# Two row additions and the norms' reciprocal roots are divided anew between VectorE and GpSimd in a two-layer graph-attention and expert kernel

## The chip, the cores and the metric

The kernel runs on one core of one Trainium2 chip. A core has five engines that run side by side, each through its own list of instructions in order: TensorE (PE in the profile; its weight loads are PEld), VectorE (DVE), ScalarE (ACT), GpSimd (POOL) and SyncE (SP). They wait for each other by semaphores. In this kernel SP issues the plain transfers, and GpSimd issues the indirect ones, that is, those whose row addresses come from a tile. The metric is the device time of one execution in microseconds; lower is better.

## What is computed

The input x has 64 batches of 256 rows with 256 values, all float32. Two layers follow, each with attention over a fixed adjacency mask and then a feed-forward part. Every part works on the row-normalised x and is added to x:

```
x = x + elu(attention(layernorm(x), adj, 4 heads))
x = x + layernorm(x) @ weight.T + bias            # the dense layer
x = x + relu(attention(layernorm(x), adj, 1 head))
x = x + moe(layernorm(x))                         # 8 experts, the best 2 of each row
layernorm(x) = (x - mean) / sqrt(var + 1e-5)
```

So each batch has four norms: of the input, before the dense layer, before the second attention, and before the experts. The mixture of experts returns `tokens + sum of weight * expert(tokens)` over the two experts that a router picks for the row.

## The kernel before, in words

**Tiles.** A batch is held as a tile of 128 partitions by 2 row blocks by 256 values, 512 float32 values in each partition. The means need no subtraction, since the weights are centred once in the setup; a norm needs only the factor `rstd = (var + eps)^-0.5` for every row. `norm_stats` gets it: VectorE takes statistics of each row block (L290, L291), and then GpSimd does two instructions on a 128x2 tile, an addition of eps (L293) and a power with -0.5 (L294).

**The steps of a batch.** `batch_layers` is a generator, and each `yield` ends a step of the batch and names the rank that the next step has among all the work of its turn. Counted from 0, the steps that matter here are: 0, norm 1 (of the input x0) and a transposition; 1, the projection to q (L315), its exponentials on ScalarE with rstd as scale (L323) and its scaling on VectorE (L327); 2 and 3, the scores z (L346); 4, the weighted sums pv (L360) and hp; 5, x1 (L394 to L398); 6, x1b, which is x1 plus the bias (L401, on GpSimd), norm 2 and a transposition of x1; 7, the dense layer pf (L408), x2 (L414) and norm 3; 8 to 11, the second attention; 12, its rows rel on ScalarE (L431) and their addition to x2 (L434, on GpSimd); 13, norm 4; 14, the small factors `by` (L440, L443); 15, the normalised rows xng for the experts and the residual base (L449, L454); then the router's logits.

**The order.** The order of all instructions is written by the loop at the end of the kernel, under a manual schedule. A new batch begins at every third turn (`TICKS = 3`), so five or six batches are in work at one time, each at another step. In each turn every active job makes one step, in the order of their ranks. Batches go in chunks of 4 (twelve times), then of 2 (six times), then of 1 (twice); the last two batches are dense, that is, every expert is computed for them. At the end of a chunk, `route` works out on VectorE where each row goes, and `send` (L741) scatters the rows to a place in memory sorted by expert: two sends for each row block, spread over the turns on GpSimd's queue.

**Experts.** A pair is 256 sorted rows for one expert. `expert_pair` loads its rows xr (L599) and the expert's weights we (L610) by SP's queue; the load of xr waits for the sends that may lie in it. A pair's next steps are the transposition px (L617), a copy to sT on ScalarE (L621), the hidden layer ph (L649) and hT (L655), and the second product py (L664), to which VectorE adds a bias into the tile y (L670). ScalarE scales y (L642), and then `scatter` adds its rows to the output by two indirect transfers from GpSimd's queue (L681). One pair is scattered in a turn, and each scatter waits for the two transfers before it. A dense expert uses the same y tiles, and adds them to its own base (L707), which SP stores in the end (L714).

**Buffers.** A tile's `bufs` says how many copies of it exist; a new one waits for the reader of the oldest. Here y has 6, the tile "e" has 2, mv has 6, and rstd has 8.

Of the kernel before, what the change touches and what calls it, by code (L numbers as in the profile page):

```python
# [8 lines left out]
F32 = mybir.dt.float32  # L9
I32 = mybir.dt.int32  # L10
AF = mybir.ActivationFunctionType
ALU = mybir.AluOpType
AX = mybir.AxisListType

P = 128
# [11 lines left out]
def kernel(  # L27
# [17 lines left out]
    nc = tc.nc  # L45
    B, N, D = x.shape
# [4 lines left out]
    NT = N // P  # L51
    EPS = 1e-5
# [54 lines left out]
    nc.vector.memset(ones, 1.0)  # L107
    mean_w = const.tile([P, P], F32, tag="mean_w", name="mean_w")
    nc.vector.memset(mean_w, 1.0 / D)
    mhalf = const.tile([P, NT], F32, tag="mhalf", name="mhalf")  # L110
    nc.vector.memset(mhalf, -0.5)

    adj_i = work.tile([P, NT, N], adj.dtype, tag="z", name="adj_i", bufs=6)
# [25 lines left out]
    def gnn_weights(w, a, heads, slope, name):  # L139

        d = D // heads
        wx = const.tile([P, KT, heads, d + 3], F32, tag=name, name=name)
        for k in range(KT):
            nc.sync.dma_start(
                out=wx[:, k, :, :d],  # L150
                in_=w[k * P : (k + 1) * P, :].rearrange("p (h d) -> p h d", h=heads),
            )
        av = work.tile([P, 2, d], F32, tag="e", name=name + "_a")
        nc.scalar.dma_start(out=av.rearrange("p s d -> p (s d)"), in_=rows_to_all(a, 2 * d))
        prod = work.tile([P, heads, d], F32, tag="hp", name=name + "_p")
        for k in range(KT):
            for s, c in ((0, d + 1), (1, d)):
                nc.vector.tensor_mul(
                    prod, wx[:, k, :, :d], av[:, s : s + 1, :].to_broadcast([P, heads, d])
                )  # L160
                nc.vector.tensor_reduce(wx[:, k, :, c : c + 1], prod, AX.X, ALU.add)
            nc.vector.tensor_scalar(
                wx[:, k, :, d + 1 : d + 2], wx[:, k, :, d + 1 : d + 2], 1.0 - slope, None,
                op0=ALU.mult,
            )
            nc.vector.tensor_scalar(
                wx[:, k, :, d + 2 : d + 3], wx[:, k, :, d : d + 1], slope - 1.0, None,
                op0=ALU.mult,
            )
        flat = wx.rearrange("p k h c -> p k (h c)")  # L170
        center(flat, heads * (d + 3))
        return flat
# [29 lines left out]


    C_B1, WROW = KT * D, KT * D + 64
    WBUFS, XBUFS = 7, 5
    wpack = tc.dram_tile([E, P, WROW], F32, name="wpack")
    w2s = const.tile([P, E, KT * D], F32, tag="w2s", name="w2s")
    b2s = const.tile([P, E, D], F32, tag="b2s", name="b2s")
# [74 lines left out]

    def norm_stats(src):
        stats = small.tile([P, NT, 6], F32, tag="stats", name="stats")
        mv = small.tile([P, NT, 2], F32, tag="mv", name="mv", bufs=6)
        for t in range(NT):
            nc.vector.bn_stats(stats[:, t, :], src[:, t, :])  # L290
            nc.vector.bn_aggr(mv[:, t, :], stats[:, t, :])  # L291
        rstd = small.tile([P, NT], F32, tag="rstd", name="rstd", bufs=8)
        nc.gpsimd.tensor_scalar_add(rstd, mv[:, :, 1], EPS)  # L293
        nc.gpsimd.tensor_tensor(rstd, rstd, mhalf, ALU.pow)  # L294
        return mv, rstd

    def transposed(src, tag="xT", bufs=4):
        pt = bank("pt", [KT, N])
# [71 lines left out]
    def batch_layers(b, c0, xng, lg):  # L370

        x0 = xin.pop(b)
        if b + AHEAD < B:
            xin[b + AHEAD] = load_batch(b + AHEAD)
        _, rstd = norm_stats(x0)
        xT = transposed(x0)
        yield 20
        q = projected(xT, wx0, H, rstd)
        yield 10
        probs = []  # L380
        scores(q, H, range(0, 2), masks[0], probs)
        yield 10
        scores(q, H, range(2, 4), masks[0], probs)
        yield 50
        pvs, rinv = attended(q, H, probs)
        hp = work.tile([P, NT, D], F32, tag="hp", name="hp")
        for t, pv in enumerate(pvs):
            nc.vector.tensor_tensor(
                hp[:, t, :].rearrange("p (h d) -> p h d", h=H), pv[:, :, :HD],
                rinv[:, t, :, None].to_broadcast([P, H, HD]), ALU.mult,  # L390
            )
        yield 20
        ex = work.tile([P, NT, D], F32, tag="e", name="e")
        nc.scalar.activation(ex, hp, AF.Exp)  # L394

        x1 = work.tile([P, NT, D], F32, tag="x1", name="x1", bufs=2)
        nc.vector.scalar_tensor_tensor(x1, hp, 0.0, x0, op0=ALU.max, op1=ALU.add)
        nc.vector.scalar_tensor_tensor(x1, ex, 1.0, x1, op0=ALU.min, op1=ALU.add)  # L398
        yield 30
        x1b = work.tile([P, NT, D], F32, tag="x1b", name="x1b")  # L400
        nc.gpsimd.tensor_add(x1b, x1, bias_f[:, None, :].to_broadcast([P, NT, D]))  # L401
        _, rstd = norm_stats(x1)
        xT = transposed(x1)
        yield 70
        pf = bank("pf", [NT, D])
        for t in range(NT):
            for k in range(KT):
                nc.tensor.matmul(  # L408
                    pf[:, t, :], xT[:, k, t * P : (t + 1) * P], wfT[:, k, :],
                    start=(k == 0), stop=(k == KT - 1),  # L410
                )
        x2 = work.tile([P, NT, D], F32, tag="x2", name="x2", bufs=4)
        for t in range(NT):
            nc.vector.scalar_tensor_tensor(  # L414
                x2[:, t, :], pf[:, t, :], rstd[:, t : t + 1], x1b[:, t, :],
                op0=ALU.mult, op1=ALU.add,
            )
        _, rstd = norm_stats(x2)
        yield 60
        xT = transposed(x2)  # L420
        yield 20
        q = projected(xT, wx1, 1, rstd)
        yield 10
        probs = []
        scores(q, 1, range(1), masks[1], probs)
        yield 40
        pvs, rinv = attended(q, 1, probs)
        yield 5
        rel = work.tile([P, NT, D], F32, tag="rel", name="rel")
        for t, pv in enumerate(pvs):  # L430
            nc.scalar.activation(  # L431
                rel[:, t, :], pv[:, 0, :D], AF.Relu, scale=rinv[:, t, :]
            )
        nc.gpsimd.tensor_add(x2, x2, rel)  # L434
        yield 60
        mv, rstd = norm_stats(x2)
        yield 15

        by = small.tile([P, 2, NT], F32, tag="by", name="by")
        nc.vector.scalar_tensor_tensor(  # L440
            by[:, 0], mv[:, :, 0], -1.0, rstd, op0=ALU.mult, op1=ALU.mult
        )
        nc.vector.tensor_scalar(by[:, 1], rstd, 1.0, None, op0=ALU.add)  # L443
        yield 50
        xe = keep.tile([P, NT, ROW], F32, tag="xng", name="xng", bufs=XNG)
        dense = b >= ROUTED
        base = work.tile([P, NT, D], F32, tag="dbase" if dense else "base", name="base")
        for t in range(NT):
            nc.scalar.activation(  # L449
                xe[:, t, :D], x2[:, t, :], AF.Identity, bias=by[:, 0, t : t + 1],  # L450
                scale=rstd[:, t : t + 1],
            )
        for t in range(NT):
            nc.scalar.activation(  # L454
                base[:, t, :], x2[:, t, :], AF.Identity, bias=by[:, 0, t : t + 1],
                scale=by[:, 1, t : t + 1],
            )
        xng.append(xe)
        yield 35
        if not dense:  # L460
            d = nc.sync.dma_start(
                out=out_rows[b * N : (b + 1) * N, :].rearrange("(t p) d -> p t d", p=P), in_=base
            )
            tc.declare_no_dep(
                d.ins, query=SYNC, group="out", reason="no row is added to before its chunk has been sent"
            )
            tc.add_to_no_dep_group("out", d.ins)
            based.append(d.ins)
            nc.sync.nop()
        xT = transposed(xe[:, :, :D], *(("xTd", DENSE) if dense else ()))  # L470
        yield 50
        pl = bank("pl", [NT, E])
        for t in range(NT):
            for k in range(KT):
                nc.tensor.matmul(
                    pl[:, t, :], xT[:, k, t * P : (t + 1) * P], rT[:, k, :],
                    start=(k == 0), stop=(k == KT - 1),
                )
        nc.vector.tensor_copy(lg[:, c0 : c0 + NT, :], pl)
        if dense:  # L480
            dense_batch[b] = dict(base=base, xT=xT)
# [178 lines left out]
    def result(hT, e):  # L660
        py = bank("py", [2, D])
        for t in range(2):
            for f in range(KT):
# [2 lines left out]
                    w2s[:, e, f * D : (f + 1) * D].rearrange("p e c -> p (e c)"),  # L666
                    start=(f == 0), stop=(f == KT - 1),
                )
        y = io.tile([P, 2, D], F32, tag="y", name="y", bufs=6)
        nc.vector.tensor_add(y, py, b2s[:, e, :].to_broadcast([P, 2, D]))  # L670
        return y

# [225 lines left out]
    with tc.manual_schedule():  # L898
        while more or active or waiting or dense_jobs or scatters:
# [22 lines left out]
            order_steps.append(step)  # L922
            for entry in sorted(active, key=lambda a: a[:2]):
                entry[0] = next(entry[2], None)
            active[:] = [a for a in active if a[0] is not None]
            step += 1

# [34 lines left out]
```

## Time and profile before

| what | us |
|---|---|
| median of 3 runs | 1796.04 (1791.09 to 1798.93) |
| the profiled execution | 1822.89 |
| its span, first to last instruction | 1821.2 |
| TensorE busy (matmuls) | 1629.5 (89%) |
| VectorE busy | 1231.4 (68%) |
| ScalarE busy | 839.9 (46%) |
| GpSimd busy | 1084.2 (60%) |
| GpSimd: the two row additions, 64 each | 109.2 and 108.1 |
| GpSimd: the norms' two instructions, 256 each | 81.2 and 184.2 |
| GpSimd: scatters (262) and sends (248) | 419.4 and 261.2 |

Lines of the profile name the source line, the engine, the operation, and the tiles as output<-input. In tables by group the numbers after a count are busy us and mean ns of one, and behind the bar the idle time just before and who ended it. A timeline line has the start, the length, the instruction, and in brackets the idle time of its engine before it and what ended that. In tables of stretches each engine has its busy us and instructions, in the order PE, PEld, DVE, ACT, POOL, and then come the granted TensorE clock (1.00 is full speed), the transfers' share and GB/s. The profiled execution was slower than the median by 26.9 us; its mean granted clock was 0.937.

### The profile page before, as it was taken

To read this page: it belongs to the slowest core of one execution; us is meant where nothing else is said; L and a number is where in the kernel's file an instruction comes from. 1 tells how busy PE (TensorE), PEld (TensorE's weight loads), DVE (VectorE), ACT (ScalarE), POOL (GpSimd) and SP (SyncE) were. 2 spreads that over 40 slices of the span, in tenths; PEclk is the share of its full clock that TensorE was granted. 3 is DMA by queue.
4 is the path that set the end of the run, shared out by engine and by line. 5 is a ranking of instruction groups with operands and counts; after the bars stand their busy time and mean duration, and the time that the engine had idled before them with its cause. 6 is when DMAs were issued, how large, how long until landed. Compare 5 with 4: busy or idle time off the path is not lost. (4 is left out here: it accounts for less than half of the span.)

```text
span 1821.2 us, 30155 instructions
## 1 busy us (share of the span) xinstructions
PE 1629.5 (89%) x9254; PEld 1433.0 (79%) x9254; DVE 1231.4 (68%) x4680; ACT 839.9 (46%) x1773; POOL 1084.2 (60%) x1164
## 2 busy tenths in 40 slices
PE   6998889899999999999999999999989998778692
PEld 5787778788888888888878788887878887667582
DVE  6889887867685858686766768688678876522231
ACT  1243333355554555554545545555455545443241
POOL 1333645557575767767676757576685767644444
PEclk9999989899998999998989999999899989889897
DMA  4410211235344444544354534444353436576663
GB/s 137 140 36 24 71 60 53 79 109 121 105 95 104 109 126 108 132 103 110 93 119 112 119 91 95 118 111 128 84 127 101 107 82 166 118 186 139 135 139 43
DMA packets 137374, 192.90 MB, mean 106 GB/s; under 512 B 18680, under 2 KB 91392, under 8 KB 137216
## 3 DMA queue, kind: packets, MB, share of 16 engines
q1 hardware_dynamic: 86592, 122.61, 22.0%
q0 software_dynamic: 49632, 67.39, 20.6%
q8 instruction: 76, 1.25, 0.3%
q10 hardware_dynamic: 992, 0.99, 0.2%
q14 instruction: 82, 0.67, 0.1%
HBM read 101.77 MB, written 89.15 MB: 105 GB/s over the span
## 5 line engine op out<-in xcount | busy, mean ns | idle before, releaser
L681 POOL DMA_INDIRECT out_dram<-y,to x262 | 419.4, 1601 | 231.1 <-DMA out_dram<-y,to 103.5
L360 PE MATMUL pv<-q,z 128*128 128x65 f32 (+1 forms) x2560 | 394.4, 314 | 5.3 <-DVE z L346 5.0
L360 PEld LDWEIGHTS pv<-q,z 128*128 128x128 f32 x2560 | 364.9, 210 | 21.1 <-DVE z L346 5.4
L293 POOL TENSOR_SCALAR rstd<-mv 128x2 f32<-128x2 f32 x256 | 81.2, 317 | 376.2 <-DVE mv L291 355.6
L741 POOL DMA_INDIRECT xs<-xng,pos x248 | 261.2, 1053 | 68.2 <-issue 66.0
L315 PE MATMUL pq<-wx,xT 128*128 128x268 f32 (+1 forms) x1024 | 265.4, 402 | 35.8 <-ACT xT L305 31.8
L649 PE MATMUL ph<-sT,we 128*128 128x256 f32 x1048 | 252.6, 397 | 48.1 <-ACT sT L621 22.9
L346 DVE SCALAR_TENSOR_TENSOR z<-pd,q,mask 128x256 f32<-128x256 f32 x640 | 265.1, 473 | 9.9 <-PE pd L339 7.5
L649 PEld LDWEIGHTS ph<-sT,we 128*128 128x128 f32 x1048 | 205.0, 200 | 80.6 <-ACT sT L621 29.4
L664 PE MATMUL py<-w2s,hT 128*128 (+1 forms) x1176 | 265.4, 381 | 0.6 <-ACT hT L655 0.6
L315 PEld LDWEIGHTS pq<-wx,xT 128*128 128x128 f32 x1024 | 188.1, 194 | 85.8 <-ACT xT L305 50.6
L664 PEld LDWEIGHTS py<-w2s,hT 128*128 128x128 f32 x1176 | 220.5, 191 | 29.3 <-ACT hT L655 1.0
L305 ACT COPY xT<-pt 128x512 f32<-128x512 f32 x256 | 144.9, 589 | 192.8 <-PE pt L301 127.6
L327 DVE SCALAR_TENSOR_TENSOR q<-pq,rstd,q 128x256 f32<-128x256 f32 x256 | 112.4, 479 | 154.5 <-ACT q L323 150.7
L655 ACT ACTIVATE hT<-ph,we 128x256 f32<-128x256 f32 x294 | 123.3, 471 | 173.4 <-PE ph L649 122.9
L670 DVE TENSOR_TENSOR y<-py,b2s 128x512 f32<-128x512 f32 x147 | 96.7, 688 | 149.2 <-PE py L664 77.9
L294 POOL TENSOR_TENSOR rstd<-rstd,mhalf 128x2 f32<-128x2 f32 x256 | 184.2, 719 | 21.4
L642 ACT ACTIVATE y<-y,w 128x256 f32<-128x256 f32 x262 | 112.9, 498 | 177.5 <-DVE y L670 171.1
L290 DVE BATCH_NORM_STATS2 stats<-x 128x6 f32<-128x256 f32 x384 | 155.9, 406 | 0.0
L408 PE MATMUL pf<-wfT,xT 128*128 128x256 f32 x512 | 145.7, 435 | 0.1
L323 ACT ACTIVATE q<-pq,rstd 128x12 f32<-128x12 f32 (+1 forms) x256 | 56.5, 265 | 162.3 <-POOL rstd L294 150.8
L434 POOL TENSOR_TENSOR x<-x,rel 128x512 f32<-128x512 f32 x64 | 109.2, 1706 | 25.2 <-ACT rel L431 25.0
(147 smaller groups left out, 2259.2 us busy)
## 6 DMA issues: line engine op xcount, KB each, us to landing
we<-wpack SPq DMA_DIRECT2D x147, 288.0 KB
xr<-xs SPq DMA_DIRECT2D x131, 260.0 KB
xin<-in_x_dram SPq DMA_DIRECT2D x64, 256.0 KB
out_dram<-base SPq DMA_DIRECT2D x64, 256.0 KB
out_dram<-y,to POOLq DMA_INDIRECT x262
xs<-xng,pos POOLq DMA_INDIRECT x248
xs<-fill SPq DMA_DIRECT2D x9, 260.0 KB
wpack<-wt SPq DMA_DIRECT2D x8, 288.0 KB
```

Source lines behind the costliest of these rows:

```text
L290: nc.vector.bn_stats(stats[:, t, :], src[:, t, :])
L294: nc.gpsimd.tensor_tensor(rstd, rstd, mhalf, ALU.pow)
L305: nc.scalar.copy(dst, pt)
L315: nc.tensor.matmul(pq.rearrange("p h c -> p (h c)"), xT[:, k, t * P : (t + 1) * P], wx[:, k, :], start=(k == 0), stop=(k == KT - 1),)
L346: nc.vector.scalar_tensor_tensor(z[:, j, :], pd[:, i, :], q[:, j, h, d + 2 : d + 3], mask[:, j, :], op0=ALU.max, op1=ALU.mult,)
L360: nc.tensor.matmul(pv[:, h, :], z[:, j, t * P : (t + 1) * P], q[:, j, h, : d + 1], start=(j == 0), stop=(j == NT - 1),)
L408: nc.tensor.matmul(pf[:, t, :], xT[:, k, t * P : (t + 1) * P], wfT[:, k, :], start=(k == 0), stop=(k == KT - 1),)
L649: nc.tensor.matmul(ph[:, f, :], we[:, k * D + f * P : k * D + (f + 1) * P], xT[:, k, :], start=(k == 0), stop=(k == KT - 1),)
L655: nc.scalar.activation(hT[:, f, :], ph[:, f, :], AF.Gelu, bias=we[:, C_B1 + f : C_B1 + f + 1])
L664: nc.tensor.matmul(py[:, t, :], hT[:, f, t * P : (t + 1) * P], w2s[:, e, f * D : (f + 1) * D].rearrange("p e c -> p (e c)"), start=(f == 0 ...
L681: d = nc.gpsimd.indirect_dma_start(out=out_rows, out_offset=bass.IndirectOffsetOnAxis(ap=to[:, t : t + 1], axis=0), in_=y[:, t, :], in_off ...
L741: d = nc.gpsimd.indirect_dma_start(out=xs_d[: E * CAP * PAIR, :], out_offset=bass.IndirectOffsetOnAxis(ap=at, axis=0), in_=xe, in_offset=None,
```

## The change

GpSimd no longer adds rows. VectorE adds the bias (x1b) in step 5, straight behind x1, and adds the second attention's rows to x2 at the start of step 13, ahead of norm 4. In `norm_stats` the first norm of a turn leaves its statistics and its rstd in the first half of a double tile, the second norm uses the other half, and then one pair of GpSimd instructions on 128x4 serves both. A norm that finds no partner in its turn is finished alone at the turn's end. Norm 2 and norm 1 of two batches fall in one turn, in that order, and norm 4 and norm 3 of two others in another. The buffers follow: mv 4 and rstd 5 of the double size, "e" 1, which in the setup also holds the two attentions' vectors one after the other, and y 7.

```
-        mv = small.tile([P, NT, 2], F32, tag="mv", name="mv", bufs=6)
+        if half_done:
+            mv, rstd = half_done[0]
+            at = NT
+        else:
+            mv = small.tile([P, 2 * NT, 2], F32, tag="mv", name="mv", bufs=4)
+            rstd = small.tile([P, 2 * NT], F32, tag="rstd", name="rstd", bufs=5)
+            half_done.append((mv, rstd))
+            at = 0
         for t in range(NT):
             nc.vector.bn_stats(stats[:, t, :], src[:, t, :])
-            nc.vector.bn_aggr(mv[:, t, :], stats[:, t, :])
-        rstd = small.tile([P, NT], F32, tag="rstd", name="rstd", bufs=8)
-        nc.gpsimd.tensor_scalar_add(rstd, mv[:, :, 1], EPS)
-        nc.gpsimd.tensor_tensor(rstd, rstd, mhalf, ALU.pow)
-        return mv, rstd
+            nc.vector.bn_aggr(mv[:, at + t, :], stats[:, t, :])
+        if at:
+            finish_norms(2 * NT)
+        return mv[:, at : at + NT, :], rstd[:, at : at + NT]
+
+    def finish_norms(n):
+        mv, rstd = half_done.pop()
+        nc.gpsimd.tensor_scalar_add(rstd[:, :n], mv[:, :n, 1], EPS)
+        nc.gpsimd.tensor_tensor(rstd[:, :n], rstd[:, :n], mhalf[:, :n], ALU.pow)
...
+        x1b = work.tile([P, NT, D], F32, tag="x1b", name="x1b")
+        nc.vector.tensor_add(x1b, x1, bias_f[:, None, :].to_broadcast([P, NT, D]))
         yield 30
-        x1b = work.tile([P, NT, D], F32, tag="x1b", name="x1b")
-        nc.gpsimd.tensor_add(x1b, x1, bias_f[:, None, :].to_broadcast([P, NT, D]))
         _, rstd = norm_stats(x1)
...
-        nc.gpsimd.tensor_add(x2, x2, rel)
         yield 60
+        nc.vector.tensor_add(x2, x2, rel)
         mv, rstd = norm_stats(x2)
...
-        av = work.tile([P, 2, d], F32, tag="e", name=name + "_a")
+        av = work.tile([P, 2, d], F32, tag="e", name=name + "_a", bufs=1)
...
-        ex = work.tile([P, NT, D], F32, tag="e", name="e")
+        ex = work.tile([P, NT, D], F32, tag="e", name="e", bufs=1)
...
-    WBUFS, XBUFS = 7, 5
+    WBUFS, XBUFS, YBUFS = 7, 5, 7
...
-        y = io.tile([P, 2, D], F32, tag="y", name="y", bufs=6)
+        y = io.tile([P, 2, D], F32, tag="y", name="y", bufs=YBUFS)
...
             for entry in sorted(active, key=lambda a: a[:2]):
                 entry[0] = next(entry[2], None)
+            if half_done:
+                finish_norms(NT)
```

More of the change, by code (lines that the diff above doesn't have):

```diff
@@ L109 @@
     nc.vector.memset(mean_w, 1.0 / D)
-    mhalf = const.tile([P, NT], F32, tag="mhalf", name="mhalf")
+    mhalf = const.tile([P, 2 * NT], F32, tag="mhalf", name="mhalf")
     nc.vector.memset(mhalf, -0.5)
@@ L280 @@
     nc.vector.memset(scan_mask[:, :, 0:1], 0.0)
+    half_done = []
     def norm_stats(src):
         stats = small.tile([P, NT, 6], F32, tag="stats", name="stats")
-        mv = small.tile([P, NT, 2], F32, tag="mv", name="mv", bufs=6)
+        if half_done:
[6 more added lines that the diff above has]
+            at = 0
         for t in range(NT):
             nc.vector.bn_stats(stats[:, t, :], src[:, t, :])
-            nc.vector.bn_aggr(mv[:, t, :], stats[:, t, :])
-        rstd = small.tile([P, NT], F32, tag="rstd", name="rstd", bufs=8)
-        nc.gpsimd.tensor_scalar_add(rstd, mv[:, :, 1], EPS)
-        nc.gpsimd.tensor_tensor(rstd, rstd, mhalf, ALU.pow)
-        return mv, rstd
+            nc.vector.bn_aggr(mv[:, at + t, :], stats[:, t, :])
[6 more added lines that the diff above has]
+        nc.gpsimd.tensor_tensor(rstd[:, :n], rstd[:, :n], mhalf[:, :n], ALU.pow)
     def transposed(src, tag="xT", bufs=4):
```

## The prediction

> **What bounds the kernel now.** I read the page's busy shares first, then a table of stages (busy us and instructions by engine, granted TensorE clock), then the waits, then the timeline around them.
>
> ```profile
> PE 1629.5 (89%) x9254; PEld 1433.0 (79%) x9254; DVE 1231.4 (68%) x4680; ACT 839.9 (46%) x1773; POOL 1084.2 (60%) x1164
> ```
> ```profile
> 20.00:350.00 330.00, 293.24 (x1733) 254.23 (x1734) 270.50 (x937) 108.85 (x259) 144.63 (x204) 0.92 0.22 66
> 350.00:1240.00 890.00, 851.86 (x5021) 757.56 (x5020) 638.11 (x2392) 476.79 (x982) 605.02 (x645) 0.96 0.45 110
> 1240.00:1590.00 350.00, 309.49 (x1706) 272.85 (x1706) 252.86 (x1124) 177.90 (x366) 233.48 (x238) 0.92 0.47 113
> 1590.00:1780.00 190.00, 157.48 (x733) 136.11 (x733) 52.80 (x170) 71.18 (x159) 80.89 (x52) 0.91 0.64 148
> ```
>
> TensorE is busy 96% from 350 to 1240 us, so nothing off it counts unless it opens or closes one of its gaps. Its clock is only 0.96 there, though: at half speed for 8% of 890 us, some 71 us, so about 36 us lost besides 38 us of gaps. In that stage the waits put 18.5 us, in 13 pieces, on px (L617) waiting for xr. This is one such piece, at the end of a chunk of four batches:
>
> ```profile
> 819.50 1.86 POOL L434 TENSOR_TENSOR x<-x,rel 128x512 f32<-128x512 f32 x1
> 820.73 1.86 POOL L401 TENSOR_TENSOR x1b<-x,bias_f 128x512 f32<-128x512 f32 x1
> ...
> 823.87 0.71 POOL L294 TENSOR_TENSOR rstd<-rstd,mhalf 128x2 f32<-128x2 f32 x1
> 824.61 0.43 ACT L323 ACTIVATE q<-pq,rstd 128x12 f32<-128x12 f32 x2 [2.04 <-POOL rstd L294]
> ...
> 824.92 0.88 DVE L327 SCALAR_TENSOR_TENSOR q<-pq,rstd,q 128x256 f32<-128x256 f32 x2 [2.71 <-ACT q L323]
> ...
> 830.08 0.22 POOL L293 TENSOR_SCALAR rstd<-mv 128x2 f32<-128x2 f32 x1 [0.75 <-DVE mv L291]
> ...
> 831.26 1.10 POOL L741 DMA_INDIRECT xs<-xng,pos  x1 [0.17 <-issue]
> ...
> 835.50 0.96 POOL L741 DMA_INDIRECT xs<-xng,pos  x1 [0.31 <-issue]
> ...
> 842.63 1.09 PE L617 MATMUL px<-ident,xr 128*128 128x128 f32 x4 [2.08 <-DMA xr<-xs]
> ```
>
> Read down: GpSimd does both row additions before the reciprocal roots, so rstd comes late; ScalarE waits 2.04 us for it, VectorE 2.71 us for ScalarE. Nothing else stops VectorE until its statistics at 829.99; GpSimd's last root and the four sends follow, SP loads xr behind the sends, TensorE waits 2.08 us. And this follows (same columns as the stage table):
>
> ```profile
> 745.00:755.00 10.00, 7.91 (x58) 7.27 (x58) 4.88 (x23) 4.55 (x10) 7.83 (x10) 1.00 0.78 202
> 835.00:843.00 8.00, 5.58 (x31) 4.38 (x30) 4.34 (x13) 4.57 (x11) 7.04 (x7) 0.97 0.84 217
> 843.00:853.00 10.00, 10.00 (x43) 9.51 (x42) 3.92 (x19) 4.02 (x8) 5.27 (x7) 0.51 0.58 128
> ```
>
> The gap is followed by 10 us at half clock: 5 us of work lost. At the boundary where the gap was 1.49 us (747.8) the clock stays at 1.00. Gaps of 1.85 us and more all drew a half-clock stretch; eight boundaries from 268 to 1146 us did, with 74 us at half speed by the clock column of such tables, so 37 us lost. (The eleven boundaries in all are these eight, 747.8, and two at 352 and 1241 us with gaps of 0.6 and 1.0 us.)
>
> [...] two tiny copies ran into the additions,
>
> ```profile
> 239.65 2.84 DVE L804 COPY r<-two 128x8 f32<-128x8 f32 x2
> ```
>
> where two take about 0.25 us elsewhere[...].
>
> **The change, part by part.** Rows used (count, busy us, mean ns):
>
> ```profile
> L434 POOL TENSOR_TENSOR x<-x,rel 128x512 f32<-128x512 f32 x64 | 109.2, 1706 | 25.2 <-ACT rel L431 25.0
> L401 POOL TENSOR_TENSOR x1b<-x,bias_f 128x512 f32<-128x512 f32 x64 | 108.1, 1689 | 7.6 <-DVE wt L212 5.6 <-PE pq L315 2.0
> L294 POOL TENSOR_TENSOR rstd<-rstd,mhalf 128x2 f32<-128x2 f32 x256 | 184.2, 719 | 21.4
> L293 POOL TENSOR_SCALAR rstd<-mv 128x2 f32<-128x2 f32 x256 | 81.2, 317 | 376.2 <-DVE mv L291 355.6
> L398 DVE SCALAR_TENSOR_TENSOR x<-e,x 128x512 f32<-128x512 f32 x64 | 44.3, 692 | 6.7
> ```
>
> *Rows.* GpSimd loses 217 us. VectorE gains 128 additions at 0.69 us (L398's shape), 88 us, and loses what the lock cost it: about 19 us, summed over instructions more than 60 ns above their own median during an addition. Net +69 us, 72% busy.
>
> *Norms.* A batch begins every third step; its norms come at its steps 0, 6, 7 and 13, so norm 1 meets norm 2 in one step, norm 3 meets norm 4 in another. 256 pairs of instructions become some 130, about 130 us saved at 1.04 us each. The power on 128x4 is not in the trace: 0.72 us if the cost is fixed, 1.42 if by element. I take 1.0.
>
> *The boundary.* New times at 820 us: x0's statistics end at 820.10, GpSimd's scatter at 820.06, so the shared pair ends by 821.5. ScalarE scales y until 822.58, then q at 822.6, not 824.61: 2.0 us earlier; VectorE follows (pv ends 823.3, so rinv isn't late). The row addition ahead of norm 4 gives 0.69 back: statistics at 828.7, pair until about 830, sends at about 830.1 instead of 831.26, so 1.2 us earlier (0.7 if the power doubles; 2.4 at 932, where VectorE waited 3.8). The gaps of 1.85 to 2.53 fall to 0.3 to 1.3. Eight times 1.2 is 10 us. I count seven tenths of the 37 us of half clock as gone, 26 us[...]. **-36 us**; bounds -55 and 0.
>
> *Before 350 us* VectorE is 82% busy. Twenty batches bring +28 us, the lock gives 10 back; its waits for q and rinv (0.7 and 1.3 us in the batch at 83 us, from the timeline there) can take up the 1.4 us that a batch brings. The 2.81 us gap at 247 and 1.07 us at 223 follow lock stalls of 2.6 and 2.9; with those gone they shrink, and 3.4 us of half clock each may. **-4**, bounds -12 and +20 (cover gone).
>
> *New waits.* Norm 4's "by" (L440) now needs norm 3's statistics: pair ready about 830.0, "by" due at 830.2. With a slow power VectorE waits up to 0.4 us there, with x1 (L397) behind it, and px(x1) behind that: 0 to +10, counted 0. The row addition on VectorE waits for rel, written a step earlier: nothing. x1b sits behind x1, ahead of rinv; the z that pv needs were 2.4 us early in the batch at 820, which hides both additions.
>
> *Setup.* The second attention vector shares one buffer, so its load waits for the last product of the first (about 10.4 us) and lands some 3 us later; products due at 11 start at about 13. bias and wf loads queue behind it on ScalarE. **+2**, bounds 0 and +5.
>
> *A seventh y.* VectorE waits 48.5 us for y buffers, all after 1600. There five y are taken for three scatters of 6.4 us each; the last of a round still needs the same scatter, so the base store at 1701.2, which blocks SP and costs TensorE 15.1 us, moves by about 1.5. **-2**, bounds -12 and +2. Other buffer counts outlast their readers: 0.
>
> Sum: -36 - 4 + 2 - 2 = -40. On the profiled execution (1822.9, span 1821.2) that gives 1783. The median, 1796.0, is 26.9 lower. The likeliest place for that excess is the same gaps and half-clock stretches, so runs outside the profiler have less to win: I take seven tenths, 28 us: **1768**.
>
> **Rivals.**
> - *A, the forecast*, 62%: 1768, own range 1745 to 1786. For it: the 2.7 us wait stands on the chain to the gap.
> - *B, hidden*, 18%: sends come earlier but the half clock still follows [...], or gaps open elsewhere and draw it. Only the 10 us of gaps less a few: 1792, from 1787 to 1801. For it: VectorE rises everywhere[...]; against it: VectorE's slack is 25% from 350 on.
> - *C, slower*, 20%: sends come later. The row addition (0.69) and a doubled power (0.70) stand on the chain, 1.4 us; if q isn't freed because ScalarE's queue holds it, eleven boundaries grow by 1.4 us, 15 us, and one or two more half-clock stretches at 5 us follow: 1816, from 1806 to 1830. It decides once the freed wait is under 1.4 us; 2.0 is what I read.
>
> **Numbers.** A difference under 0.5% (9 us) is about what measurement can't tell. Faster: A and a sixth of B, 65%. Same: most of B, some of A, 14%. Slower: C and a bit of B, 21%. The range 1745 to 1808 leaves out most of C and A's low end.
>
> **What would show it.** Right: no GpSimd addition, q's wait for rstd near zero, px gaps under 1.3 us and a mean clock above 0.96 from 350 on. Wrong: gaps at px kept or moved to pt or pv behind VectorE; the power above 1.2 us; half-clock stretches as many as before.

## The result and the profile after

The changed kernel takes 1767.15 us (median of 4 runs, 1761.69 to 1771.5) where the kernel before, beside it, takes 1793.64: a ratio of 0.985, 95% interval 0.981 to 0.989. Measured again later, in the second lot of runs below, the ratio was 0.991 (0.988 to 0.994). So the forecast of 1768 was met in sign and size, and the size was in part luck. The profiled execution is 1771.5 us long, 51 less than that of before.

Busy shares of the changed kernel, and its stages (busy us and instructions of PE, PEld, DVE, ACT and POOL, then the granted clock, the transfers' share and GB/s):

```profile
PE 1584.4 (90%) x9254; PEld 1394.4 (79%) x9254; DVE 1296.0 (73%) x4808; ACT 834.6 (47%) x1773; POOL 838.8 (47%) x788
```
```profile
20.00:350.00 330.00, 284.88 (x1730) 242.95 (x1729) 278.41 (x960) 104.26 (x251) 78.77 (x104) 0.95 0.21 65
350.00:1240.00 890.00, 860.91 (x5231) 769.77 (x5230) 720.40 (x2602) 494.86 (x1029) 482.89 (x447) 0.99 0.46 116
1240.00:1590.00 350.00, 312.19 (x1722) 273.58 (x1721) 243.68 (x1088) 179.59 (x370) 195.93 (x172) 0.94 0.53 133
```

VectorE gained 65 us and GpSimd lost 245. ("The lock" in the recorded texts is only a name for what was measured: VectorE's instructions ran longer beside a row addition, in the profile of before by 19.3 us in all. Why they did isn't shown.) From 350 to 1240 us the clock went from 0.96 to 0.99, and TensorE's gaps from 38 to 29 us. In the waits of that stage (us, times, longest) px fell from 18.5 us to the first line, and ScalarE's wait for rstd from 59.9 to the second:

```profile
PE px L631 <- DMA xr<-xs: 5.9, 5, 2.2
ACT q L337 <- POOL rstd L309: 6.6, 8, 2.1
```

A boundary in the timeline of the changed kernel, in the batch that begins at 811.8; it answers to that shown of before, whose batch began at 819:

```profile
813.35 1.04 POOL L309 TENSOR_TENSOR rstd<-rstd,mhalf 128x4 f32<-128x4 f32 x1
...
815.22 0.41 ACT L337 ACTIVATE q<-pq,rstd 128x12 f32<-128x12 f32 x2
...
821.76 1.04 POOL L309 TENSOR_TENSOR rstd<-rstd,mhalf 128x4 f32<-128x4 f32 x1
...
823.00 1.09 POOL L755 DMA_INDIRECT xs<-xng,pos  x1 [0.20 <-issue]
824.40 0.98 POOL L755 DMA_INDIRECT xs<-xng,pos  x1 [0.30 <-issue]
...
827.08 1.48 SPq L613 DMA_DIRECT2D xr<-xs  x3
...
833.81 0.63 PE L631 MATMUL px<-ident,xr 128*128 128x128 f32 x4 [1.48 <-DMA xr<-xs]
```

The shared root takes 1.04 us, q follows without a wait for it, the first send leaves 11.2 us into the batch, and the gap is 1.48 us instead of 2.08. No half-clock stretch follows it: the clock is 1.00 from 835 to 855.

Where the 51 us went, by the starts of batches in the two profiled executions: up to batch 20, 374 us became 380; batches 20 to 48, 695 became 661; batches 48 to 63, 385 became 365; the rest, 367 became 364.

### The profile page after: what moved, and what is told of

It reads as the page before. It is cut to its first block, busy times and chain, and to the rows that moved or that the text cites. A ratio compares the mean times of both kernels' runs of the same rounds, so it can differ in the third digit from the quotient of the medians.

```text
span 1769.8 us, 29975 instructions
## 1 busy us (share of the span) xinstructions
PE 1584.4 (90%) x9254; PEld 1394.4 (79%) x9254; DVE 1296.0 (73%) x4808; ACT 834.6 (47%) x1773; POOL 838.8 (47%) x788
## 5 line engine op out<-in xcount | busy, mean ns | idle before, releaser
L374 PE MATMUL pv<-q,z 128*128 128x65 f32 (+1 forms) x2560 | 366.3, 298 | 8.0 <-DVE y L684 8.0
L374 PEld LDWEIGHTS pv<-q,z 128*128 128x128 f32 x2560 | 337.2, 195 | 23.4 <-DVE y L684 10.0
L329 PE MATMUL pq<-wx,xT 128*128 128x268 f32 (+1 forms) x1024 | 269.2, 407 | 35.2 <-ACT xT L319 35.2
L308 POOL TENSOR_SCALAR rstd<-mv 128x4 f32<-128x4 f32 (+1 forms) x132 | 43.4, 329 | 518.0 <-DVE mv L301 450.0
L755 POOL DMA_INDIRECT xs<-xng,pos x248 | 250.7, 1011 | 69.1 <-issue 67.7
L309 POOL TENSOR_TENSOR rstd<-rstd,mhalf 128x4 f32<-128x4 f32 (+1 forms) x132 | 135.7, 1028 | 10.9
L422 PE MATMUL pf<-wfT,xT 128*128 128x256 f32 x512 | 132.0, 403 | 0.0
L353 PE MATMUL pd<-ident,q 128*128 128x128 f32 x640 | 105.3, 280 | 10.5 <-ACT q L337 10.5
L408 ACT ACTIVATE e<-hp 128x512 f32<-128x512 f32 x64 | 40.3, 630 | 155.9 <-DVE hp L402 155.9
```

What stands on the lines that cost most here:

```text
L309: nc.gpsimd.tensor_tensor(rstd[:, :n], rstd[:, :n], mhalf[:, :n], ALU.pow)
L329: nc.tensor.matmul(pq.rearrange("p h c -> p (h c)"), xT[:, k, t * P : (t + 1) * P], wx[:, k, :], start=(k == 0), stop=(k == KT - 1),)
L374: nc.tensor.matmul(pv[:, h, :], z[:, j, t * P : (t + 1) * P], q[:, j, h, : d + 1], start=(j == 0), stop=(j == NT - 1),)
L422: nc.tensor.matmul(pf[:, t, :], xT[:, k, t * P : (t + 1) * P], wfT[:, k, :], start=(k == 0), stop=(k == KT - 1),)
L755: d = nc.gpsimd.indirect_dma_start(out=xs_d[: E * CAP * PAIR, :], out_offset=bass.IndirectOffsetOnAxis(ap=at, axis=0), in_=xe, in_offset=None,
```

## The experiments

Twelve runs in three lots, each on one chip with runs of the kernel before beside it: 1815.0 us in the first lot, 1811.0 in the second, 1803.1 in the third. Only ratios can be compared between lots; the expected times below were worked out from the 1796 us of the kernel before, so against a slower chip they are read as ratios too. In the diffs the lines are those of the kernel that the text names.

### One half of the change at a time

The kernel before once more:

> The kernel before, unchanged, profiled once more, because its first profiled execution lay 27 us above the median. Theory (the chain from rstd to the sends, with the half clock behind the gap): an execution near 1794 us shows the same gaps at px, at least six of eleven above 1.5 us, and 45 to 70 us at half clock between 350 and 1240 us. Rival (the first profile was only a disturbed one): gaps under 1 us and a clock of 0.99 there, and the change's gain must lie elsewhere.

1809.1 us, one run; the profile shows 16.8 us in 14 waits of px for xr from 350 to 1240 us, five of TensorE's gaps there above 1.5 us, and 48 us of half clock where the first profile had 65. The stretches are a property of the kernel, but their number isn't fixed.

Only the additions moved (the kernel before, norms unshared, old buffers):

```
-        yield 30
         x1b = work.tile([P, NT, D], F32, tag="x1b", name="x1b")
-        nc.gpsimd.tensor_add(x1b, x1, ...)
+        nc.vector.tensor_add(x1b, x1, ...)
+        yield 30
...
-        nc.gpsimd.tensor_add(x2, x2, rel)
         yield 60
+        nc.vector.tensor_add(x2, x2, rel)
```

> The kernel before with the two row additions on VectorE at their new places; each norm keeps its own two GpSimd instructions, and all buffers stay. Theory (chain): two single pairs still end by about the time that ScalarE has scaled y, so q is freed as in the change, and all of the gain is here: 1764 to 1774 us. Rival (the halved number of GpSimd instructions does it): 1785 us or more.

1766.0 us, ratio 0.975 (0.968 to 0.981). The theory's range is 0.982 to 0.988 as a ratio, so the additions alone won more than it said.

Only the shared norms (the changed kernel, both additions back on GpSimd at their old places, y 6, e 2):

```
-        nc.vector.tensor_add(x1b, x1, ...)
         yield 30
+        nc.gpsimd.tensor_add(x1b, x1, ...)
...
+        nc.gpsimd.tensor_add(x2, x2, rel)
         yield 60
-        nc.vector.tensor_add(x2, x2, rel)
```

> The change with both row additions back on GpSimd at their old places, and with the old buffer counts: only the shared pair of norm instructions is new. Theory (chain): the additions still stand ahead of the shared pair, which ends only 0.7 to 1.0 us earlier; a third of the gain, 1778 to 1790 us. Rival (pairing does it): 1765 to 1772 us. [...]

1811.3 us, ratio 0.997 (0.993 to 1.000): not the third of the gain that the theory gave it (as a ratio 0.990 to 0.997, of which the measurement meets only the end), and not told apart from no gain at all. And the whole change with the old buffers:

```
-    WBUFS, XBUFS, YBUFS = 7, 5, 7
+    WBUFS, XBUFS, YBUFS = 7, 5, 6
-        ex = work.tile([P, NT, D], F32, tag="e", name="e", bufs=1)
+        ex = work.tile([P, NT, D], F32, tag="e", name="e")
```

(and the same for the setup's vectors).

> The change with y back at six buffers and the tile e at two, so that the attention vectors are loaded side by side again. Theory (chain): both only move the edges, by +2 for y and -2 for the setup: 1765 to 1770 us, no measurable difference from the change. Rival (the seventh y frees the tail): 1775 us or more.

1781.0 us, ratio 0.981 (0.974 to 0.988), where the theory's range is 0.983 to 0.986: no difference from the change is shown. So the whole gain sits in the additions. Sharing the norms brings nothing measurable alone, and with the additions the kernel that shares is 15 us slower than the one that doesn't; the intervals of the ratios overlap, but no run of the one (four, from 1771.6 us) is as short as any of the other (four, up to 1770.7). The second lot asked that again.

### Does sharing cost?

> The changed kernel once more, beside the three below, so that they have a neighbour on the same chip. Every theory: a ratio to the kernel before of 0.975 to 0.987.

1791.6 us, ratio 0.991 (0.988 to 0.994): above the expected band. In this lot px still waits 13.4 us for xr, in ten pieces, from 350 to 1240 us.

The changed kernel with `norm_stats` of before:

```
-        if at:
-            finish_norms(2 * NT)
...
+        rstd = small.tile([P, NT], F32, tag="rstd", name="rstd", bufs=8)
+        nc.gpsimd.tensor_scalar_add(rstd, mv[:, :, 1], EPS)
+        nc.gpsimd.tensor_tensor(rstd, rstd, mhalf, ALU.pow)
```

> The changed kernel with norm_stats as before: every norm has its own two GpSimd instructions on 128x2; the additions stay on VectorE, y has 7 buffers, e has 1. Theory 'sharing costs' (a shared pair starts only when the later of its two norms has its statistics, and the longer power of 1.05 us stands in that path): 5 to 15 us faster than the changed kernel beside it. Rival 'sharing is free or helps' (132 fewer instruction pairs, 1.04 us each, and GpSimd's sends earlier for it): within 5 us of it, or slower by up to 10 us.

1781.4 us, ratio 0.984 (0.978 to 0.991): 10 us faster than the changed kernel beside it. The intervals overlap a little, but both lots have the sign and about the size. VectorE's waits from 1240 to 1590 us show a place for it, in the changed kernel first and then in the kernel with the additions alone:

```profile
DVE by L454 <- POOL rstd L309: 16.7, 3, 9.8
```
```profile
DVE by L440 <- POOL rstd L294: 3.6, 2, 2.3
```

Norm 4's `by` now waits until the partner's statistics are in, up to 9.8 us (11.5 us in three waits in the profile of the second lot). With unshared norms beside the changed kernel's buffers this wait doesn't occur at all in that stage.

### Moving the sends, aimed wrong

Two more powers, which nobody reads, in the changed kernel. By `t == nt - 2` they stand ahead of the last pair of sends but one, not of the last pair, as the expectation has it:

```
+            if not last and t == nt - 2:
+                for _ in range(2):
+                    nc.gpsimd.tensor_tensor(idle_t, idle_t, mhalf, ALU.pow)
             for k in range(2):
                 send(...)
```

> The changed kernel with two more powers on a 128x4 tile that nobody reads (1.05 us each) on GpSimd's queue just ahead of the last pair of sends of a chunk but for the last chunk, so that those sends come some 2 us later; VectorE's work is the same. Theory 'time of the sends' (what was won is that the sends of a chunk's end come earlier): the waits of px for xr open again at 1 to 3 us each and draw half clock, 20 to 45 us slower than the changed kernel beside it. Rival 'VectorE freed of the lock' (what was won is VectorE's own time, and the sends only look late): within 5 us of it.

1826.2 us, ratio 1.006 (1.002 to 1.010): 35 us slower than the changed kernel beside it, for 2.1 us on GpSimd's queue per chunk (38 powers, 38.8 us in all) of which VectorE has no part. The size is the first theory's, the waits are not: half clock from 350 to 1240 us rose from 17 to 48 us, waits of px for xr only from 13.4 to 15.0. The powers also hold up the scatters and roots behind them, so this run doesn't show that the loss goes by the sends.

Two of the last four sends ahead of the norms (the kernel before):

```
-                yield from later(95)
+                yield from later(58 if t == nt - 3 else 95)
```

> The kernel before with one rank changed: the last pair of sends but one of a chunk runs ahead of its turn's norms on GpSimd's queue (rank 58 for 95), so that two of the last four sends have left when the last two begin, about 1 us earlier for the last. Additions, norms and buffers are as before. Theory 'time of the sends': px waits shrink by about 1 us at each boundary, 8 to 25 us faster than the kernel before. Rival 'VectorE freed of the lock': within 5 us of it, or slower by some us since the norms of that turn wait behind two sends.

1790.9 us, ratio 0.988 (0.982 to 0.995). The size was as expected and the reason was not. Px's waits fell to 2.7 us, but TensorE now waits elsewhere in the same stage,

```profile
PE pt L301 <- DVE z L346: 18.9, 9, 2.5
```

in a kernel whose norms 4 and 3 of that turn now stand behind two sends; half clock there is 75 us, and batches 20 to 48 take 682 us, not less than the 674 of the kernel before run again. The gain came after batch 48, and why is open.

Both runs also showed that I had the wrong sends. In the order of the compiled program, a chunk's last two pairs of sends are the ones apart from each other (in the trace of before those at 805.81 and 812.84); the four at 831.26, in front of the gap at 842.63, are the *first* of the next chunk. Yet the loads of xr wait for them. In every batch's time, at a boundary or not, the first load of xr left after that batch's second send, mostly 2.6 to 3.6 us (4.5 at most); and in the program each such load waits for the last send placed before it. At the boundary of before that is the second of the four:

```profile
832.67 1.25 POOL L741 DMA_INDIRECT xs<-xng,pos  x1 [0.30 <-issue]
835.63 2.16 SPq L599 DMA_DIRECT2D xr<-xs  x3
```

So a load waits not only, as the description of the kernel has it, for the sends that may lie in its pair. The waits of SP's queue in the kernel before, from 350 to 1240 us, had it all along:

```profile
SPq L599 <- DMA xs<-xng,pos: 430.2, 26, 19.4
```

26 waits and 430 us, up to 19.4 us each, so SP stands in most batches, not at the ends of chunks alone. A pair needs rows of the finished chunk only, and at 835.63, where the loads leave, the last of those had been sent 21 us before.

### GpSimd's queue, or what its additions cost VectorE?

With the additions on VectorE, GpSimd got its time back in two ways: by a power on a 128x8 tile that nobody reads, or by an addition of 128x512 into a tile that nobody reads, at each of the two old places.

```
+        nc.gpsimd.tensor_tensor(idle_t, idle_t, mhalf8, ALU.pow)
         _, rstd = norm_stats(x1)
...
+        nc.gpsimd.tensor_tensor(idle_t, idle_t, mhalf8, ALU.pow)
         yield 60
         nc.vector.tensor_add(x2, x2, rel)
```

(and `tensor_add(idle_t, idle_t, bias_f)` in the other).

> Both additions on VectorE (norms and buffers as before), but GpSimd spends about the time that they took: at each of their two old places it raises a 128x8 tile that nobody reads to a power (1.7 us, worked out from 0.72 us for 128x2 and 1.05 us for 128x4). Theory 'GpSimd's queue' (the gain is that the roots, sends and scatters behind the additions come earlier): hardly any gain is left, ratio to the kernel before 0.995 to 1.015. Rival 'lock' (the gain is that GpSimd's wide additions no longer stop VectorE): the gain of the moved additions stays, ratio 0.97 to 0.985.

1821.0 us, ratio 1.010 (1.005 to 1.015): nothing of the gain is left.

> As the kernel with the powers, but GpSimd makes a 128x512 addition of the bias into a tile that nobody reads at each of the two old places, so it keeps both its queue's time and what VectorE loses beside such an addition; VectorE does the real additions. Theory 'GpSimd's queue': as slow as the kernel with the powers, within 10 us. Rival 'lock': slower than that kernel by 20 to 45 us. Against the kernel before both say the same or slower, ratio 1.00 to 1.03.

1842.5 us, ratio 1.021 (1.017 to 1.026). GpSimd's groups in the two kernels (busy us, mean ns):

```profile
L439 POOL TENSOR_TENSOR idle_t<-idle_t,mhalf 128x8 f32<-128x8 f32 x64 | 135.5, 2117 | 0.2
L406 POOL TENSOR_TENSOR idle_t<-idle_t,mhalf 128x8 f32<-128x8 f32 x64 | 105.3, 1645 | 4.9
```
```profile
L437 POOL TENSOR_TENSOR idle_t<-idle_t,bias_f 128x512 f32<-128x512 f32 x64 | 109.5, 1712 | 0.2
L404 POOL TENSOR_TENSOR idle_t<-idle_t,bias_f 128x512 f32<-128x512 f32 x64 | 84.1, 1314 | 4.9
```

The powers took 241 us, not the 217 that the additions took before, so this kernel gives GpSimd 11% too much. With them, ScalarE waits 83.0 us for rstd from 350 to 1240 us (59.9 before), and TensorE's gaps there grow to 52 us. So GpSimd's time alone, almost without longer instructions on VectorE, undoes the gain; how much of that goes by the roots, and how much by the sends and scatters behind them, isn't separated. VectorE's instructions that overlap with a power, 636 of them, are in sum no longer than their own medians (-0.5 us); the 449 that overlap with such an addition are 32.7 us above. The same instruction from 20 to 350 us, in the kernel with the powers and then in that with the additions:

```profile
L402 DVE SCALAR_TENSOR_TENSOR x<-e,x 128x512 f32<-128x512 f32 x17 | 11.8, 692 | 2.1 <-DVE x L401 0.5
```
```profile
L400 DVE SCALAR_TENSOR_TENSOR x<-e,x 128x512 f32<-128x512 f32 x16 | 16.3, 1019 | 1.7
```

The additions make the kernel 21.5 us slower than the powers do (20 to 45 were expected), although they hold GpSimd 47 us less. In the profiles, one of each kernel, that loss lies early, where VectorE is busy 83 to 84% (20 to 350 us): batch 20 starts at 404 us, not at 379, and batches 20 to 48 take 686 us in either. So there are two costs in a GpSimd addition here: its queue time, with which alone the ratio is 1.010, and the longer instructions of VectorE beside it, 32.7 us in the profile and felt in the first 350 us.

### The loads of xr ahead of the sends

The first theory's cause was a load that waits behind sends. Now the sends of a batch's time all go at the end of its last turn, behind the loads that this turn issues. In the kernel before:

```
-        yield from later(95)
+        yield 95
+        while not last and (len(order_steps) - 1) % TICKS != 2:
+            yield 95
         mark = len(sent)
...
-            if not last:
-                yield from later(95)
-            elif t % 2:
+            if t % 2:
                 yield 95
+                while not last and t < nt - 1 and (len(order_steps) - 1) % TICKS != 2:
+                    yield 95
```

> The kernel before with the sends of rows placed otherwise: the two pairs of sends that a batch's time holds both go at the end of its last turn, behind the loads of xr that this turn issues, so that a load of xr waits for the sends of a batch earlier alone. In the traces so far every first load of xr leaves 2.6 to 3 us after the second send of its own batch's time, sends of the next chunk among them. Additions, norms and buffers are as before. Theory 'sends hold up xr': the waits of px for xr (18 us from 350 to 1240 us) and the half clock after them go, 15 to 35 us faster than the kernel before. Rival 'the roots are late': TensorE's gaps come at pt, pd or pv in their place, within 8 us of the kernel before.

1751.4 us, ratio 0.971 (0.966 to 0.975): with GpSimd's additions, unshared norms and roots that still come late, it is 52 us faster than the kernel before, more than the 15 to 35 expected, and its interval lies wholly below that of the change. The timeline at a boundary, and the stage from 350 to 1240 us:

```profile
790.04 1.50 SPq L599 DMA_DIRECT2D xr<-xs  x3
...
800.66 1.10 POOL L741 DMA_INDIRECT xs<-xng,pos  x1 [0.18 <-issue]
```
```profile
350.00:1240.00 890.00, 864.49 (x5290) 776.88 (x5289) 680.17 (x2556) 505.66 (x1037) 631.11 (x680) 0.99 0.47 116
```

The loads leave 11 us ahead of the batch's sends. No wait of px for xr is left in that stage, half clock there is 14 us, TensorE's gaps are 26 us (9.6 of them a new wait of pf for q), and ScalarE still waits 45 us for rstd. The rival "the roots are late" allowed 8 us. So late roots did harm in the kernel before mostly by making the sends, and with them xr, late. The fall of ScalarE's wait from 59.9 to 45 us may be the new placing's work too, and what it is worth isn't separated. Later still, as with the powers, roots seem to do harm of their own.

The same in the kernel with VectorE's additions and unshared norms:

> The same placing of the sends in the kernel with VectorE's additions and unshared norms (y 7, e 1). Both theories: not slower than that kernel's ratio of 0.984; where the sends hold up xr, its 13.6 us of waits of px for xr go too, ratio 0.965 to 0.98; where the roots are late, 0.98 to 0.99.

1755.7 us, ratio 0.973 (0.968 to 0.978), not told apart from the line above it. Once xr doesn't wait for the sends, moving the additions gains nothing measurable: batch 20 starts at 379 us instead of 369, and batches 20 to 48 take 654 instead of 646.

The chain in one table: medians over the first seven of the nine batches from 350 to 1240 us in which a chunk's first three pairs are loaded, in us from that batch's start, and two sums from 350 to 1240 us.

| kernel | first send | first xr | px waits for xr | half clock | ratio |
|---|---|---|---|---|---|
| before | 12.3 | 17.2 | 18.5 | 65 | 1 |
| before, profiled again | 12.2 | 16.8 | 16.8 | 48 | 1 |
| norms shared alone | 12.6 | 16.8 | 13.9 | 51 | 0.997 |
| additions alone | 10.9 | 15.3 | 9.9 | 7 | 0.975 |
| the change, as first shown | 11.1 | 15.3 | 5.9 | 24 | 0.985 |
| the change, second lot | 11.1 | 15.4 | 13.4 | 17 | 0.991 |
| additions, powers in their place | 13.6 | 18.3 | 9.8 | 17 | 1.010 |
| before, loads first | 10.6 | 0.4 | 0 | 14 | 0.971 |

The row with the powers doesn't fit a single cause: half clock is short there though the sends are late, and part of the loss is new gaps at pd and pf, which wait for q (9.0 and 5.1 us).

## Why the prediction was right, step by step

- **The boundary** (-36 us). The edit's times came as worked out: the first send left 1.2 us earlier in its batch (12.34 to 11.14, the prediction said 1.2), q some 2 us earlier, px's gaps fell from 18.5 to 5.9 us and the half clock from 65 to 24 (that seven tenths of it would go was an estimate; 41 us went). Batches 20 to 48 gained 34 us. In the two profiles taken again they took 674 and 670 us, a gain of 4 with 48 and 17 us of half clock, so this step's size differs from one execution to another by as much as the whole effect.
- **What failed in that step** is "the four sends follow, SP loads xr behind the sends" as a fact of a chunk's end. They were the next chunk's sends, whose rows the pair doesn't need, and the loads waited for the first two of them because they stand after these in the program; with the loads placed ahead, 52 us went. The prediction took a wait for a need; the waits of SP's queue would have shown it.
- **Norms** ("about 130 us saved at 1.04 us each"). GpSimd saved about 86 us: 265 us became 179, since a shared pair takes 1.05 + 0.32 us on 128x4. The power was sized right (1.0 for 1.05); the saving was worked out at the old price. It bought nothing: unshared sends leave 10.8 to 10.9 us into the batch, shared ones 11.1.
- **New waits** ("0 to +10, counted 0"). VectorE's wait of `by` is 4.8 us from 350 to 1240 us and 16.7 from 1240 to 1590. The likely price of sharing, 10 to 15 us by two comparisons, was counted at its lower end.
- **Before 350 us** (-4). Batch 20 started 6 us later, at 380; in the kernel before run again it was 382, so no difference is shown. What GpSimd's additions cost by VectorE's longer instructions is real, 25 us in one pair of profiles when they are put back beside the moved ones, where the prediction had 10, and being rid of it about pays for the 28 that it counted for the moved additions.
- **Setup and the seventh y** (+2, -2). Batch 1 starts at 32 and 33 us in the changed kernel, at 29 and 30 in the two with VectorE's additions and two e; so the setup came as said. What follows batch 63's start gained 3 us, but the seventh y isn't shown to have brought it: with six it took 361 us in the change with the old buffers, with seven 364 and 360.
- **Left out of the sum**: batches 48 to 63, -20 us (-14 in the profiles taken again). The prediction priced the boundaries of chunks of four and no stage after 1240 us, where the chain is the same: VectorE's wait for q falls there from 24.3 to 10.6 us and ScalarE's for rstd from 16.8 to 6.4, and with the powers in place they are 27.6 and 20.1 and the stage takes 391 us. That lost time on GpSimd's queue costs this stage is shown. Half clock there fell from 55 to 41 us (62 to 51 in the profiles taken again), 7 and 6 us of work, so it carries a part of the gain only.
- **From profile to median**: 51 us between the profiles became 26.5 between the medians, half and not seven tenths. The unpriced -20 and the missed discount cancelled, which is luck, and is why 1768 lies 1 us from the result.
- **The rivals.** *Hidden* expected gaps elsewhere; that happened where sends were moved in front of norms, not in the change. *Slower* needed a freed wait below 1.4 us, and q came some 2 us earlier.
- **The signs** that it named were met in part: ScalarE's wait for rstd is 6.6 us, the power 1.05, and the clock from 350 us to 1240 is 0.99, but from 1240 to 1590 it is 0.94, and gaps at px of 1.48 and 2.2 us remain, not all under 1.3.

## What to carry to other kernels

When a transfer waits, ask of what it needs before asking how to make its producer faster: here the first load of xr in every batch's time waited for a send placed before it (at the boundary shown, one whose rows it didn't need) and left mostly 2.6 to 3.6 us behind it, and changing the order of the two was worth at least as much here (ratio 0.971) as all the additions taken off the engine in front (0.975). Read the waits of the queue that issues the transfers, not only those of the engine that starves. Work that is taken off a queue should be tested with the same time put back, once with and once without the suspected side effect.

## What the runs showed that I had not expected

- GpSimd's power took longer on a wider tile, 0.72 us on 128x2, 1.05 on 128x4, 1.65 on 128x8 (2.1 at the other place), and didn't lengthen what VectorE did beside it (-0.5 us over 128 powers on 128x8); 128x512 additions of 1.3 to 1.7 us did (32.7 us over 128).
- The length of a gap doesn't decide alone whether half clock follows. Gaps of 1.85 us and more all drew one in the first profile of before, from 350 to 1240 us, but at 222.85 one of 1.07 us did too, and at 1652.70 one of 2.62 us did not; in the kernel with shared norms alone a gap of 2.45 us drew none and one of 1.10 us did (the clock of the 10 us after each stands in the stretches):

```profile
457.45 1.40 PE L631 MATMUL px<-ident,xr 128*128 128x128 f32 x8 [2.45 <-DMA xr<-xs]
745.93 0.63 PE L631 MATMUL px<-ident,xr 128*128 128x128 f32 x4 [1.10 <-DMA xr<-xs]
```
```profile
455.00:465.00 10.00, 7.41 (x55) 6.92 (x56) 5.04 (x24) 4.68 (x10) 7.48 (x7) 1.00 0.90 233
747.00:757.00 10.00, 10.00 (x41) 9.18 (x41) 4.57 (x21) 4.28 (x8) 4.03 (x3) 0.50 0.54 118
```

What decides it beside the length isn't shown.
- Two microseconds on one queue, once a chunk, 39 us in all, cost 35 us; a change of order alone gained 52.
- The same two kernels differed by 1.5% in one comparison and by 0.9% in another.
